# Giving each DMA engine its own partitions in the split x loads of a pairwise bilinear kernel

## Chip, cores and metric

The kernel runs on one core of one Trainium2 chip. The metric is the device time of one execution in microseconds (us). The core has a matrix engine (TensorE, in the profile PE), VectorE (DVE), ScalarE (ACT), GpSimd (POOL) and SyncE (SP); ACT, POOL and SP here only issue DMA transfers, apart from four constants that POOL writes at the start. The transfers of all three run on the same 16 DMA engines, numbered 0 to 15.

## What is computed

For 4096 samples with 32 fields of 64 numbers each, every pair of fields (i < j, 496 pairs) has its own 64 x 64 matrix W; the result is the product of field i with that matrix, multiplied elementwise with field j.

```python
i_idx, j_idx = np.triu_indices(32, k=1)
vi = inputs[:, i_idx, :]            # (4096, 496, 64)
vj = inputs[:, j_idx, :]
vdotw = jnp.einsum('bpd,pde->bpe', vi, W)
out = (vdotw * vj).reshape(4096, -1)
```

All is in float32. The output is 520 MB, the inputs together 42 MB.

## The kernel before

**Tiling.** The 4096 samples are cut into 8 chunks of 512 (`BANK`). The host puts x into a layout where a field pair is one block of 128 partitions (two fields of 64) by 512 samples; there are 16 such blocks. W lies in SBUF for the whole run, loaded at the start by SP in five pieces. For each chunk the steps (`steps_of`) go through the blocks in four groups of four (`GROUP`): first the pairs inside a group's blocks (L206), then each block p of the group with the later blocks q (L216). The matmuls write PSUM banks, VectorE multiplies them with x (L226, L234) and writes into one of three SBUF slots of 20, 18 and 18 blocks of 512 columns. When a slot is full SP stores it (L179): 4.6 or 5.1 MB per transfer. The next use of a slot waits for its store.

**The x loads.** x of a chunk is in one SBUF buffer of 128 partitions, half of it blocks 0 to 7, half blocks 8 to 15. Once the second group of a chunk is done, nothing in that chunk reads the first half again, and the first half of the next chunk is loaded there, while groups three and four go on; the second half follows after the last group. A half is 128 rows of 16 KB, 2 MB. As a rule a half is one transfer from ACT with all 128 partitions (L140), called a whole load here.

**The four split loads.** In chunks 1, 3, 5 and 7 (`LIGHT_CHUNKS`) the first half is loaded by `load_beside` instead, so that DMA engine 4 (`LIGHT`) moves none of its rows. It consists of two transfers from POOL: one over 15 engines, from engine 5 on and around to engine 3, 8 rows each (`HEAD`), partitions 0 to 119 in order; and one over two engines, 4 rows each (`REST`), partitions 120 to 127. The pair of engines changes from load to load (`PAIRS_FROM`: 7 and 8, 15 and 0, 1 and 2, 7 and 8). In DRAM the host writes one line for each engine, with 16 numbers (`PAD`) of padding behind it.

**Which engine a POOL transfer starts at.** [...] `from_engine(e)` moves this position: it issues a tiny transfer over as many engines as are to be skipped, called a nudge, into one of two small tiles that nothing reads. A nudge is issued as early as its place in POOL's order allows, which is the order of the program. So POOL's queue, for each split load, is: (nudge, issued long before) pair, nudge, the 15 engine transfer, nudge for the next split load.

**Order around the change.** ACT issues nothing but x loads, in program order, SP only W and the stores. Each waits on semaphores for the work that last read or wrote its place. A transfer takes a completion semaphore from a small rotating set, one set of eight for ACT and SP together, one of eight for POOL, and waits until the semaphore's last user is complete.

Of the kernel before, what the change touches and what calls it, by code (L numbers as in the profile page):

```python
# [8 lines left out]
F32 = mybir.dt.float32  # L9
ALU = mybir.AluOpType  # L10

P = 128
# [7 lines left out]
DMA_ENGINES = 16  # L20
LIGHT = 4
LIGHT_CHUNKS = [1, 3, 5, 7]
PAIRS_FROM = [7, 15, 1, 7]
HEAD = P // DMA_ENGINES
REST = HEAD // 2
PAD = 16


# [33 lines left out]
def is_light(load):  # L62

    return load[1] == 0 and load[0] in LIGHT_CHUNKS


def load_size(load):

    pads = (DMA_ENGINES + 1) * PAD if is_light(load) else 0
    return P * (load[2] - load[1]) * GROUP * BANK + pads  # L70


# [1 line left out]
def pair_bilinear_kernel(  # L74
# [10 lines left out]
    nc = tc.nc  # L85
# [5 lines left out]
    const = ctx.enter_context(tc.tile_pool(name="const", bufs=1))  # L91
    psum = ctx.enter_context(tc.tile_pool(name="ps", bufs=1, space=bass.MemoryType.PSUM))

    nudges = [const.tile([DMA_ENGINES, 16], F32, tag=f"nudge{i}", name=f"nudge{i}") for i in range(2)]
    cursor = 0

    def from_pool(out, in_):

        tc.keep_in_program_order(nc.gpsimd.dma_start(out=out, in_=in_))  # L99

    def from_engine(e):

        nonlocal cursor
        k = (e - cursor) % DMA_ENGINES
        if k:
            nudge = nudges[e == LIGHT + 1]
            from_pool(
                nudge[:k].rearrange("p (h c) -> p h c", h=2)[:, :, :4],
                x[: k * 8].rearrange("(p h c) -> p h c", p=k, h=2),
            )  # L110
        cursor = e

    def load_beside(at, xt, n_row, lap):

        nonlocal cursor
        most = DMA_ENGINES - 1
        for e, k, rows, p in (
            (PAIRS_FROM[lap], 2, REST, most * HEAD),
            (LIGHT + 1, most, HEAD, 0),
        ):  # L120
            from_engine(e)
            n = rows * n_row
            lines = x[at : at + k * (n + PAD)].rearrange("(k c) -> k c", k=k)
            from_pool(xt[p : p + k * rows], lines[:, :n])
            at += k * (n + PAD)
            cursor = (e + k) % DMA_ENGINES

    xbuf = const.tile([P, NPR * BANK], F32, tag="x", name="x")
    loads = x_loads(B, NPR)
# [1 line left out]
    def load_x(load):  # L131

        at = sum(load_size(before) for before in loads[: loads.index(load)])
        c, g0, g1 = load
        n = (g1 - g0) * GROUP * BANK
        xt = xbuf[:, g0 * GROUP * BANK : g0 * GROUP * BANK + n]
        if is_light(load):
            load_beside(at, xt, n, LIGHT_CHUNKS.index(c))
        else:
            nc.scalar.dma_start(out=xt, in_=x[at : at + P * n].rearrange("(p c) -> p c", p=P))  # L140

    for load in loads:
        if load[0] == 0:
            load_x(load)
# [40 lines left out]
    for c in range(NC):  # L185
        todo = list(enumerate(steps))
        while todo:
            if made == base + room:
                turn += 1
                base, room = made, SLOTS[turn % len(SLOTS)]  # L190
                tag = f"slot{turn % len(SLOTS)}"
                osb = ring.tile([P, room * BANK], F32, tag=tag, name=tag)
            (s, (p, q)), rest = todo[0], todo[1:]
            n = 1
# [28 lines left out]
            if q is None:  # L223
                for h in range(2):
                    rows = slice(h * D, (h + 1) * D)
# [21 lines left out]
            for load in loads:  # L247
                if last and load[0] == c + 1 and load[2] == p // GROUP + 1:
                    load_x(load)
# [55 lines left out]
```

## Time and profile before

| | us |
|---|---|
| median of 3 runs (1312.45 to 1314.46) | 1313.95 |
| the profiled execution | 1313.7 |
| its span in the profile | 1311.9 |
| VectorE busy | 1152.9 |
| PE busy | 1061.7 |
| a split load, POOL's issue to landing: the 15 engine transfer | 31.1 to 32.6 |
| the same: the pair | 12.1 to 13.9 |
| a whole 2 MB load from ACT, issue to landing, median | 20.9 |
| a 4.6 MB store, issue to landing, median | 23.6 |
| POOL's first transfer of each split load is issued at | 124.67, 447.29, 765.93, 1089.13 |
| the first matmul of the chunk that needs it starts at | 167.74, 491.37, 810.90, 1133.99 |

How to read it: the page gives busy time per engine over the span, the span in 40 slices, and the DMA queues (q1 is SP's, q10 ACT's, q0 POOL's; "instruction" is the fetching of the program itself). A stretch is a window of the span, given in us from its start, with the busy time of each engine, the share of the 16 DMA engines' time that was in use and the bytes moved per time. Landing is the time from a transfer's issue to its completion. The trace holds a record for every packet of every DMA queue, with its start, duration and size, but without the number of its engine; each row of a transfer here is one packet.

### The profile page before, as it was taken

The numbers are of one execution on the slowest core, as the hardware profiler recorded it, in microseconds if no ns is written. First come the engines' busy times: TensorE is split into PE (matmuls) and PEld (weight loads), VectorE is DVE, ScalarE is ACT, GpSimd is POOL, SyncE is SP. The second block draws the span as 40 slices with busy tenths as digits, with TensorE's granted clock in tenths as the row PEclk, the third lists the DMA queues.
The fourth block names the chain that finished last, engine by engine and source line by source line (L and its number), as shares of the span: only waits on it lengthen the run. The fifth ranks groups of instructions, "written<-read, shape, count | busy, mean of one in ns | idle before, by whom it ended". The sixth has DMA issues, their size and how long they took to land.

```text
span 1311.9 us, 9391 instructions
## 1 busy us (share of the span) xinstructions
PE 1061.7 (81%) x4096; PEld 402.1 (31%) x4096; DVE 1152.9 (88%) x725; POOL 9.4 (1%) x20
## 2 busy tenths in 40 slices
PE   6788778888878888799777887788888888878882
PEld 2333223333333323333233322233333333323330
DVE  6998789998899879999889987899889998899993
POOL 0000000000000000000000000000000000000000
PEclk9999899998999989999899998999989999999996
DMA  9999999999999999999999999999999999999998
GB/s 391 428 440 431 421 431 432 433 431 435 433 433 431 431 429 433 430 431 430 432 432 436 434 424 423 434 433 432 432 430 434 436 430 424 432 428 435 433 429 368
DMA packets 19625, 562.39 MB, mean 429 GB/s; under 512 B 2688, under 2 KB 2688, under 8 KB 2816
## 3 DMA queue, kind: packets, MB, share of 16 engines
q1 hardware_dynamic: 16560, 528.23, 93.6%
q10 hardware_dynamic: 1872, 25.17, 4.5%
q0 software_dynamic: 1152, 8.39, 1.6%
q8 instruction: 32, 0.52, 0.1%
q14 instruction: 9, 0.07, 0.0%
HBM read 41.68 MB, written 520.09 MB: 428 GB/s over the span
## 4 chain that ended last, share of the span: by engine, by line
DMA 56%; DVE 33%; PE 7%; issue 2%; DVEq 0%
DMA out_dram<-slot 56%; DVE slot L234 30%; PE pring L216 6%; DVE slot L226 3%; PE pring L206 1%; DMA x<-in_x_dram 1%; DVEq L234 0%; DVEq L295 0%; DVEq L226 0%
## 5 line engine op out<-in xcount | busy, mean ns | idle before, releaser
L234 DVE TENSOR_TENSOR slot<-pring,x 128x1024 f32<-128x1024 f32 (+1 forms) x661 | 1077.2, 1697 | 120.8 <-DMA out_dram<-slot 75.3
L216 PE MATMUL pring<-x,w 64*128 64x512 f32 x3840 | 997.3, 628 | 212.4 <-DVE slot L234 202.9
L216 PEld LDWEIGHTS pring<-x,w 64*128 64x128 f32 x3840 | 385.7, 191 | 822.1 <-DVE slot L234 503.2
L226 DVE TENSOR_TENSOR slot<-pring,x 64x1024 f32<-64x1024 f32 x64 | 77.9, 1217 | 16.0 <-PE pring L206 15.5
L206 PE MATMUL pring<-x,w 64*64 64x512 f32 x256 | 67.8, 652 | 12.9 <-DMA x<-in_x_dram 7.7
L206 PEld LDWEIGHTS pring<-x,w 64*64 64x64 f32 x256 | 16.4, 143 | 62.2 <-issue 30.2
L99 POOL DMA_DIRECT2D x<-in_x_dram x8 | 4.7, 586 | 1080.3 <-DVE slot L234 759.9
L99 POOL DMA_DIRECT2D nudge<-in_x_dram x8 | 4.6, 569 | 0.9 <-POOLq L291 0.9
L291 POOL MEMSET const-bfloat16-1.0<- 128x1 bf16 x1 | 0.1, 101 | 0.0
L291 POOL MEMSET const-float32-0.0<- 128x1 f32 x1 | 0.1, 98 | 0.2 <-issue 0.2
L291 POOL MEMSET const-float32-1.0<- 128x1 f32 x1 | 0.1, 98 | 0.0
L291 POOL MEMSET const-uint8-127<- 128x1 uint8 x1 | 0.1, 98 | 0.0
## 6 DMA issues: line engine op xcount, KB each, us to landing
out_dram<-slot SPq DMA_DIRECT2D x68, 4608.0 KB, 23.6
out_dram<-slot SPq DMA_DIRECT2D x35, 5120.0 KB, 22.6
x<-in_x_dram ACTq DMA_DIRECT2D x11, 2048.0 KB, 20.9
out_dram<-slot SPq DMA_DIRECT2D x4, 2560.0 KB, 21.6
x<-in_x_dram POOLq DMA_DIRECT2D x4, 1920.0 KB, 31.6
out_dram<-slot SPq DMA_DIRECT2D x2, 2048.0 KB, 22.7
w<-in_w_dram SPq DMA_DIRECT2D x1, 2816.0 KB, 30.0
x<-in_x_dram ACTq DMA_DIRECT2D x2, 1024.0 KB, 9.2
```

Source lines behind the costliest of these rows:

```text
L99: tc.keep_in_program_order(nc.gpsimd.dma_start(out=out, in_=in_))
L206: nc.tensor.matmul(pm[o * D : (o + 1) * D, ts(k, BANK)], w_sb[m * D : (m + 1) * D, s * P + k * D : s * P + (k + 1) * D], x_of(pair, m), st ...
L216: nc.tensor.matmul(pm[:, ts(2 * i + k, BANK)], w_sb[m * D : (m + 1) * D, ts(s + i, P)], x_of(p, m), start=True, stop=True,)
L226: nc.vector.tensor_tensor(strided(osb[rows, a : a + BANK], [BANK, 2]), strided(pm[rows, :BANK], [BANK, 2]), strided(x_of(p + 1 - h, h), [2 ...
L234: nc.vector.tensor_tensor(strided(osb[:, a : a + BANK], *blocks_of), strided(pm[:, :BANK], *blocks_of), strided(x_of(q), [BANK, n], [0, 2] ...
L291: nc = bacc.Bacc("TRN2", target_bir_lowering=False, num_devices=1)
```

## The change

Each of the four split loads now has eight parts in place of two, the same in all four. The engines 5 to 7 and 8 to 15 get, from POOL, [...] in two parts each (one per block of four partitions): 5 to 7 with three engines and 12 partitions, 8 to 15 with eight engines and 32 partitions. Engines 0 to 3 get theirs in two parts from ACT, four engines and 16 partitions each. Engine 4's eight partitions go two rows each to engines 7 and 8 (48 to 51, from POOL, first) and to a last two engine transfer from ACT (16 to 19). `PAIRS_FROM`, `HEAD` and `REST` go, and so does the argument `lap`.

The order per load is: POOL pair, ACT part, POOL nudge of 12, POOL 5 to 7, POOL 8 to 15, ACT part, POOL nudge of 5, POOL 5 to 7, POOL 8 to 15, ACT pair, and then a nudge of 7 for the next split load. There are thus three nudges per load, eight POOL transfers and three from ACT; before, two nudges, four POOL transfers and none from ACT. The nudges take their target in turn from three tiles. The host writes one padded line per engine and part: 34 lines per split load, before 17. The instructions of PE and VectorE, and the order of SP's stores, stay as they were.

```diff
-PAIRS_FROM = [7, 15, 1, 7]
-HEAD = P // DMA_ENGINES
-REST = HEAD // 2
+REST_FROM = 7
+QUAD = 4
...
+def light_parts():
+
+    own = LIGHT * QUAD
+    parts = [(REST_FROM, 2, own + P // 4, QUAD // 2)]
+    for p in (0, P // 4):
+        parts.append((None, LIGHT, p, QUAD))
+        parts.append((LIGHT + 1, 7 - LIGHT, p + own + QUAD, QUAD))
+        parts.append((8, 8, p + P // 2, QUAD))
+    parts.append((None, 2, own, QUAD // 2))
+    return parts
...
-    nudges = [const.tile([DMA_ENGINES, 16], F32, tag=f"nudge{i}", name=f"nudge{i}") for i in range(2)]
-    cursor = 0
+    nudges = [const.tile([DMA_ENGINES, 16], F32, tag=f"nudge{i}", name=f"nudge{i}") for i in range(3)]
+    cursor = turns = 0
...
-            nudge = nudges[e == LIGHT + 1]
+            nudge = nudges[turns % len(nudges)]
+            turns += 1
...
-    def load_beside(at, xt, n_row, lap):
+    def load_beside(at, xt, n_row):
 
         nonlocal cursor
-        most = DMA_ENGINES - 1
-        for e, k, rows, p in (
-            (PAIRS_FROM[lap], 2, REST, most * HEAD),
-            (LIGHT + 1, most, HEAD, 0),
-        ):
-            from_engine(e)
+        for e, k, p, rows in light_parts():
             n = rows * n_row
-            lines = x[at : at + k * (n + PAD)].rearrange("(k c) -> k c", k=k)
-            from_pool(xt[p : p + k * rows], lines[:, :n])
+            lines = x[at : at + k * (n + PAD)].rearrange("(k c) -> k c", k=k)[:, :n]
             at += k * (n + PAD)
-            cursor = (e + k) % DMA_ENGINES
+            if e is None:
+                nc.scalar.dma_start(out=xt[p : p + k * rows], in_=lines)
+            else:
+                from_engine(e)
+                from_pool(xt[p : p + k * rows], lines)
+                cursor = (e + k) % DMA_ENGINES
...
-            k = (DMA_ENGINES - 1) * HEAD
-            for part in (rows[k:].reshape(2, -1), rows[:k].reshape(DMA_ENGINES - 1, -1)):
-                x.append(np.pad(part, ((0, 0), (0, PAD))).ravel())
+            for _, k, p, n in light_parts():
+                x.append(np.pad(rows[p : p + k * n].reshape(k, -1), ((0, 0), (0, PAD))).ravel())
```

More of the change, by code (lines that the diff above doesn't have):

```diff
@@ L64, in is_light @@
     return load[1] == 0 and load[0] in LIGHT_CHUNKS
+def light_parts():
[7 more added lines that the diff above has]
+    return parts
 def load_size(load):
-    pads = (DMA_ENGINES + 1) * PAD if is_light(load) else 0
+    pads = sum(k for _, k, _, _ in light_parts()) * PAD if is_light(load) else 0
     return P * (load[2] - load[1]) * GROUP * BANK + pads
@@ L101, in from_engine @@
     def from_engine(e):
-        nonlocal cursor
+        nonlocal cursor, turns
         k = (e - cursor) % DMA_ENGINES
         if k:
-            nudge = nudges[e == LIGHT + 1]
+            nudge = nudges[turns % len(nudges)]
+            turns += 1
             from_pool(
@@ L137, in load_x @@
         if is_light(load):
-            load_beside(at, xt, n, LIGHT_CHUNKS.index(c))
+            load_beside(at, xt, n)
         else:
```

## The prediction

> **What bounds the kernel now.** I read the page first (engine shares, the slices, the queues), then the stretches around the four split x loads, then the waits of VectorE, then the landings, and last the packet records of the DMA queues.
>
> ```profile
> span 1311.9 us, 9391 instructions
> PE 1061.7 (81%) x4096; PEld 402.1 (31%) x4096; DVE 1152.9 (88%) x725; POOL 9.4 (1%) x20
> ...
> DMA  9999999999999999999999999999999999999998
> GB/s 391 428 440 431 421 431 432 433 431 435 433 433 431 431 429 433 430 431 430 432 432 436 434 424 423 434 433 432 432 430 434 436 430 424 432 428 435 433 429 368
> DMA packets 19625, 562.39 MB, mean 429 GB/s; under 512 B 2688, under 2 KB 2688, under 8 KB 2816
> ...
> q1 hardware_dynamic: 16560, 528.23, 93.6%
> q10 hardware_dynamic: 1872, 25.17, 4.5%
> q0 software_dynamic: 1152, 8.39, 1.6%
> q8 instruction: 32, 0.52, 0.1%
> ```
>
> The 16 DMA engines are full in every slice but the last; VectorE is at 88%. So the end is set by the DMA engine that finishes last, and each byte is moved once already. What is left is packets that take longer than they need, and engines that end at different times. The stretches show the first (columns: busy of PE, weight loads, VectorE, POOL, TensorE clock, DMA share, GB/s):
>
> ```profile
> 130.00:160.00 30.00, 22.90 (x81) 8.17 (x82) 23.91 (x16) 0.00 (x0) 0.90 1.00 420
> 200.00:280.00 80.00, 68.80 (x284) 27.00 (x280) 78.04 (x48) 0.00 (x0) 0.99 1.00 433
> 1094.00:1124.00 30.00, 23.96 (x88) 9.50 (x88) 23.88 (x16) 0.00 (x0) 1.00 1.01 424
> 1300.00:1306.00 6.00, 0.00 (x0) 0.00 (x0) 0.00 (x0) 0.00 (x0) 0.50 0.87 375
> 1306.00:1312.00 6.00, 0.00 (x0) 0.00 (x0) 0.00 (x0) 0.00 (x0) 0.50 0.25 107
> ```
>
> The engines are as busy in the first and third row as in the second, but move 420 and 424 GB/s, not 433: those are two of the four split loads. The last rows are the engines ending one after the other.
>
> The packet records say which. A 36,864 B store row takes 1364 ns, a 16,384 B load row 611 ns, almost always. The excess over that, summed over all engines, is 13.3, 3.1, 11.2 and 10.5 us during the four split loads, and 0.2 to 3.8 us (mean 1.7) during the ten later whole loads. A packet starts about 3 ns before its engine's previous one ends, and every store gives each engine eight rows, so the packets can be chained into 16 engines; the load and nudge packets tell which is which. Ends, in us before the last one:
>
> ```
> engine                        end        extra work in the whole run
> 4 (no split load rows)        0.0        its store rows take about 24 ns longer each, 20 us in all
> eight of 5,6,9 to 14          0.0, 2.2 to 4.2    four 16 KB instruction packets each, some 1.33 us apiece
> 7, 8                          1.5, 3.2   8 rows each, 4.9 us
> 0, 1, 2, 15                   4.1 to 5.3 4 rows each, 2.4 us
> 3                             2.6        none
> ```
>
> Within the split loads engine 4 lost 4.0 us, the other engine that ends last 2.7, the rest 0.7 to 2.8.
>
> [...] during a split load store rows and POOL's packets alternate, and even a 4-byte POOL packet waits one store row.
>
> **The change, part by part.**
>
> *Bytes.* The same 2 MB per load, engine 4 still has none. Engines 7, 8, 0, 1 get two rows more per load than the others: 4 x 2 x 0.61 = 4.9 us each. Engines 7 and 8 had that already; 0 and 1 go from 2.4 to 4.9; 2 and 15 from 2.4 to 0. None of 0, 1, 7, 8 gets instruction packets (four times 1.33 = 5.3 us), so no engine has more work than the fullest had.
>
> [...] If the excess falls to that of whole loads, 38.1 - 4 x 1.7 = 31 us goes, 1.9 us for each engine. What counts is the last ones. The instruction engine that ended last would end 2.7 us earlier, the others with their own split-load loss taken off 4.5 us or more before the old end; 7 and 8 about 4.0 to 4.5; engines 0 and 1 ended 4.1 to 5.3 us before, get back 1.8 to 2.7 and take 2.4 of new rows: 3.4 to 6 us before. Engine 4 is the open one: partitions 16 to 19 and 48 to 51[...] are still written by others, now 7 and 8 together and then 0 and 1, eight rows a load as before. [...] I take 2.5: the average foreign row in all cost 38.1/512 = 0.07 us, which would be 2.4 us for 32 rows. So engine 4 ends 1.5 us earlier and stays last.
>
> *Small packets.* From POOL a DMA puts on every engine outside it as many 4-byte packets as the engines in it get rows, and one more at its end. Before: pair 4+1, nudge 1+1, the big one 8+1 and the next nudge. After, on engines 8 to 15 until the last x part has landed: 3 for the pair, 2, 5, 1, 2, 5, 1 small ones (19) and 8 rows. Each small packet takes its engine some 6 ns net, and there are 11 to 19 more per load: 0.3 to 0.5 us, on every engine. I take 0.35.
>
> *Landing.* The first row starts 5.9 us after the issue. Turns: small 1.37 us, row 1.98 us. Before: 5.9 + 8 x 1.37 + 8 x 1.98 = 32.7; the DMA answers for the windows of two of the loads say 31.1 and 32.6 (KB, us to landing):
>
> ```profile
> x<-in_x_dram POOLq DMA_DIRECT2D x1, 1920.0 KB, 31.1
> ...
> x<-in_x_dram POOLq DMA_DIRECT2D x1, 1920.0 KB, 32.6
> ```
>
> The timeline has the next chunk's first matmuls, the waits have VectorE's (us in all, times, longest):
>
> ```profile
> 167.74 1.93 PE L206 MATMUL pring<-x,w 64*64 64x512 f32 x8
> ```
> ```profile
> DVE slot L234 <- DMA out_dram<-slot: 75.3, 48, 5.3
> ```
>
> After: 5.9 + 19 x 1.37 + 8 x 1.98 = 47.7 us. POOL issues at 124.67, and the next chunk's first matmul is at 167.74, 43.1 us later (44 to 45 in the other three). So where the load was 11 us early, PE now waits 3 to 5 us for x, and VectorE behind it nearly as long. This costs the end nothing as long as the stores in flight cover it: a store lands 23 us after its issue and takes about 10.8 us of the engines, so some 12 us of older stores stand ahead of it, and VectorE, which now waits 75.3 us in all for stores (last line), makes up 4 us in about one slot cycle.
>
> *Waits and issues.* ACT's three parts wait for the same VectorE and PE work as POOL's first, then each for a completion semaphore last used by a store several stores back. Behind them on ACT stands only the whole load some 45 us later. They take three of the eight semaphores that SP's stores also use in turn; the first store to reuse one is the fifth after, over 40 us later, when a part with ten rows (a whole load: eight rows in 20.9 us) is long in. POOL issues eight DMAs at 0.57 us, not four; nothing follows on it, but 2.3 us more belongs to the landing's upper end. The third nudge target only keeps a nudge from waiting for the last; nothing waits for it. PE and VectorE instructions are unchanged, SP's order too.
>
> **Sum.** 4.0 - 2.5 - 0.35 = 1.15 us off the profiled execution (1313.7 us, span 1311.9 and 1.8 around it); the median of the runs shown is 1313.95, so 1312.8.
>
> **Rivals.**
> - *Full gain.* Engine 4 loses next to nothing to its eight foreign rows, and the last engines end 2.5 to 4 us sooner: 1310.0 to 1311.5, say 1310.8. For it: whole loads show little excess in several cases. Against: engine 4's stores are the one place where foreign rows stay.
> - *No gain.* [...] 1313.5 to 1317.5, say 1315. For it: in the fourth load, where engine 7 was one of the pair, engine 4 lost half of its 4.0 us.
> - *Slower: the late load.* The place is the start of every other chunk; the price is the stall beyond what stores in flight cover. It decides from a landing about 55 us after the issue (44 + 11). If POOL's eight DMAs or three queues on an engine stretch it to 57, each of four loads costs 2 us: 1321. For it: the landing grows by half in my own count. Against: 7 us are left, and the first engines to run dry are not the last ones.
> - *Other engines than meant.* If ACT's parts fell on engine 4, up to 40 rows x 0.61 = 24 us more on the last engine: 1337. [...]
>
> **How the numbers follow.** The forecast 0.52, full gain 0.27, no gain 0.11, late load 0.08, other engines 0.02. This kernel can tell about 0.2%, 2.6 us, from no change, that is 1311.3 to 1316.6. Faster: 0.24 of full gain, and 0.06 of the forecast where engine 4 keeps 1 us or less. Slower: 0.10 and 0.02 of no gain. Same: the rest, 0.58. The range takes in full gain and no gain, 1309.8 to 1317; late load and wrong engines are left out.
>
> **What would show it.** Right: excess in the split loads near that of whole ones, except on engine 4's stores; stretches at 430 GB/s or more; the last x part landing 45 to 50 us after POOL's issue and a PE wait of 3 to 5 us on x at four chunk starts; VectorE waiting less for stores and more for PE. Wrong: excess unchanged[...], a DMA share under 1.00 after a chunk start (the late load), load rows on engine 4.

## The result, and the profile after

The changed kernel takes 1323.24 us (median of 6 runs, 1322.76 to 1324.85), the kernel before 1312.57 (6 runs, 1311.16 to 1314.46). The ratio is 1.0082, with a 95% interval of 1.0069 to 1.0095: 10.7 us slower. The forecast was 1312.8, the range ended at 1317.0. The profiled execution has 1323.3 us and a span of 1321.5, 9.6 us more than before.

These are the lines of the page of the changed kernel that answer to those shown of before: span and engines, DMA share and GB/s in 40 slices, packets, and the queues (packets, MB, share of 16 engines).

```profile
span 1321.5 us, 9454 instructions
PE 1064.7 (81%) x4096; PEld 407.0 (31%) x4096; DVE 1153.2 (87%) x725; POOL 18.0 (1%) x36
...
DMA  9999999999999999999999999999999999999998
GB/s 391 439 430 429 427 422 430 433 421 435 425 437 430 420 427 419 431 433 423 430 423 436 430 422 422 427 432 429 424 428 427 429 435 423 422 433 431 435 429 353
DMA packets 20513, 562.39 MB, mean 426 GB/s; under 512 B 3576, under 2 KB 3576, under 8 KB 3704
...
q1 hardware_dynamic: 16560, 528.23, 93.5%
q10 hardware_dynamic: 2056, 27.53, 5.0%
q0 software_dynamic: 1856, 6.04, 1.2%
q8 instruction: 32, 0.52, 0.1%
```

The bytes are the same and the 16 engines are as full as before, yet they move 426 GB/s, not 429. So no engine stood idle; packets took longer. 888 packets more are small ones (3,576 for 2,688 under 512 B).

Where they took longer is seen in stretches. First two of the kernel before (498 to 514 us and 982 to 998 us), each for the most part inside a whole load, which the change doesn't touch; columns as in the prediction, the last two being DMA share and GB/s:

```profile
498.00:514.00 16.00, 14.07 (x56) 5.29 (x57) 16.00 (x11) 0.00 (x0) 1.00 1.02 436
...
982.00:998.00 16.00, 13.75 (x56) 5.47 (x53) 15.54 (x10) 0.00 (x0) 0.96 1.02 434
```

Then the changed kernel: a split load, a quiet stretch with stores alone, the same two stretches with whole loads, a split load again, and the end.

```profile
130.00:160.00 30.00, 22.43 (x80) 7.63 (x78) 22.27 (x16) 0.00 (x0) 0.89 1.00 425
...
200.00:280.00 80.00, 66.19 (x274) 25.16 (x274) 76.39 (x48) 0.00 (x0) 1.00 1.00 432
498.00:514.00 16.00, 15.23 (x50) 6.04 (x46) 11.51 (x8) 0.00 (x0) 0.77 1.00 415
...
982.00:998.00 16.00, 13.01 (x54) 5.44 (x54) 15.00 (x11) 0.00 (x0) 1.00 1.00 404
...
1094.00:1124.00 30.00, 25.52 (x88) 12.49 (x84) 23.68 (x15) 3.87 (x7) 0.89 1.01 423
...
1306.00:1312.00 6.00, 0.00 (x0) 0.00 (x0) 0.00 (x0) 0.00 (x0) 0.50 0.98 423
1312.00:1318.00 6.00, 0.00 (x0) 0.00 (x0) 0.00 (x0) 0.00 (x0) 0.50 0.53 225
```

The quiet stretch is as fast as before (432 for 433). Most of the loss is in the whole loads, 415 and 404 GB/s for 436 and 434, at a DMA share of 1.00: transfers that the change left as they were.

The size of these differences is rough. A packet counts where it starts, so that one store row on each engine, 16 x 36,864 B, is 37 GB/s of a stretch of 16 us, and the second load starts 9 us later in the changed kernel (987 for 978 us). A rate from the packet records is free of such edges: the bytes of all packets that start during the ten later whole loads, over the time of these packets per engine. It is 428.9 GB/s before and 417.9 after; from here on it is called the rate of the ten loads.

The packet records give it in numbers. "Excess" is, as in the prediction, the time of packets over what one of their size usually takes, summed over 16 engines; from here on only packets at least 80 ns over are counted, the start of the kernel with the load of W is left out, and 390 ns is taken off for each instruction packet that falls in (the store row behind one takes 368 to 412 ns longer). In one execution each:

```
excess, us                        before    after
in the four split loads             31.6     51.1
in the ten later whole loads        14.6     99.9
elsewhere                            3.8     15.1
```

The sum grows from 50.0 to 166.1 us, 7.3 us for each engine, and the small packets add 0.5 us to each (32.2 for 24.4 us over 16 engines). That is most of 9.6 us. Mostly store rows are hit: of 8,704 rows of 36,864 B, 251 are 80 ns or more over 1364 ns, before 99. The median stays at 1364 ns.

The waits for x and for the stores, in us in all, times, longest; first PE's wait for x in the kernel before, then both in the changed one:

```profile
PE pring L206 <- DMA x<-in_x_dram: 7.7, 1, 7.7
...
DVE slot L245 <- DMA out_dram<-slot: 81.0, 46, 5.5
...
PE pring L217 <- DMA x<-in_x_dram: 16.0, 5, 7.6
```

Of the 16.0 us, 7.6 are the wait at the start of the kernel, which was there before (7.7); 8.4 are new, at the four chunk starts that the split loads feed (2.0, 3.8, 2.4 and 0.2).

### The profile page after: what moved, and what is told of

Its sections match the earlier page's. It is cut to its first block, busy times and chain, and to the rows that moved or that the text cites. A ratio compares the mean times of both kernels' runs of the same rounds, so it can differ in the third digit from the quotient of the medians.

```text
span 1321.5 us, 9454 instructions
## 1 busy us (share of the span) xinstructions
PE 1064.7 (81%) x4096; PEld 407.0 (31%) x4096; DVE 1153.2 (87%) x725; POOL 18.0 (1%) x36
## 2 busy tenths in 40 slices
DMA packets 20513, 562.39 MB, mean 426 GB/s; under 512 B 3576, under 2 KB 3576, under 8 KB 3704
## 3 DMA queue, kind: packets, MB, share of 16 engines
q10 hardware_dynamic: 2056, 27.53, 5.0%
q0 software_dynamic: 1856, 6.04, 1.2%
## 4 chain that ended last, share of the span: by engine, by line
DMA 55%; DVE 34%; PE 6%; issue 2%; POOL 1%; DVEq 0%
DMA out_dram<-slot 41%; DVE slot L245 32%; DMA x<-in_x_dram 14%; PE pring L227 5%; DVE slot L237 2%; PE pring L217 1%; POOL x L110 1%; POOL nudge L110 0%; DVEq L245 0%; DVEq L305 0%
## 5 line engine op out<-in xcount | busy, mean ns | idle before, releaser
L227 PEld LDWEIGHTS pring<-x,w 64*128 64x128 f32 x3840 | 389.8, 192 | 816.8 <-DVE slot L245 498.3
L217 PE MATMUL pring<-x,w 64*64 64x512 f32 x256 | 73.8, 657 | 22.5 <-DMA x<-in_x_dram 16.0
L110 POOL DMA_DIRECT2D x<-in_x_dram x20 | 11.1, 564 | 1080.4 <-DVE slot L245 757.6
```

The lines of the kernel that those rows point to most:

```text
L217: nc.tensor.matmul(pm[o * D : (o + 1) * D, ts(k, BANK)], w_sb[m * D : (m + 1) * D, s * P + k * D : s * P + (k + 1) * D], x_of(pair, m), st ...
L227: nc.tensor.matmul(pm[:, ts(2 * i + k, BANK)], w_sb[m * D : (m + 1) * D, ts(s + i, P)], x_of(p, m), start=True, stop=True,)
```

## The experiments

Each ran together with the kernel before on one chip. Ratios are to it, with 95% intervals; excess is of one execution. An expectation that names a letter means: Q, partly filled transfers on ACT's queue disturb what follows; A, the addresses in DRAM (the padding); S, where tiles start in SBUF. Which partitions are an engine's own is an assumption of the author: the record of a packet names neither its engine nor its partitions.

### First round: ACT's transfers, padding, filling

**Three small ACT transfers in the kernel before.** Per split load three of them, over 4, 4 and 2 engines, into three small tiles of their own.

```diff
+    sides = [const.tile([4, 16], F32, tag=f"side{i}", name=f"side{i}") for i in range(3)]
...
+        for side, k in zip(sides, (4, 4, 2)):
+            tc.keep_in_program_order(nc.scalar.dma_start(
+                out=side[:k].rearrange("p (h c) -> p h c", h=2)[:, :, :4],
```

> The kernel before, with three tiny transfers from ACT (4, 4 and 2 engines, 64 B a row, into tiles that nothing reads) at each split load. Theory Q (a transfer from ACT over fewer than 16 engines changes how ACT's later whole loads are spread): the excess over the usual packet duration in the ten whole loads rises from 15 us, summed over engines, to about 100 us, and the time by some 5 us to 1318. Theory A (where the rows of x lie in DRAM, moved by the padding, decides the excess): no change, 1313, excess of the whole loads under 25 us.

Measured: 1.0064 [1.0047, 1.0081], whole-load excess 64.6 us. It looked like a proof that ACT's partial transfers are the cause. It was none, as the second round shows.

**Padding.** `PAD` 32 in the kernel before gives its lines the total padding of the change; `PAD` 8 in the changed kernel gives that of before.

```diff
-PAD = 16
+PAD = 32
```

> The kernel before with PAD 32 in place of 16, so that each split load carries 2176 B of padding, as in the changed kernel, and what follows in DRAM lies where it does there. Theory A: the excess in the whole loads rises to about 100 us and the time to about 1318 to 1320. Theory Q: no change, 1313.

> The changed kernel with PAD 8 in place of 16: 1088 B of padding for each split load, as in the kernel before, so that the whole loads read the same addresses as before. Theory A: the excess in the whole loads falls from 100 us to about 15 to 25 us and the time from 1323 to about 1316. Theory Q: no change, 1323.

Measured: 0.9998 [0.9987, 1.0008] and 1.0066 [1.0051, 1.0081]. The padding makes no difference beyond these intervals (the change itself: 1.0082 [1.0069, 1.0095]).

**Filling up.** The changed kernel with one more ACT transfer per split load, over six engines, so that the engines counted by ACT's partial transfers come to 16.

```diff
+    side = const.tile([6, 16], F32, tag="side", name="side")
```

> The changed kernel with one more tiny transfer from ACT over 6 engines at the end of each split load, so that the engines of ACT's partial transfers of a load add up to 16. Theory Q, if ACT's next transfer starts where the last ended: the whole loads' excess falls to about 15 us and the time to about 1316. Theory A: no change, 1323, whole loads at 100 us.

Measured: 1.0071 [1.0056, 1.0086], whole-load excess 108.5 us. No help.

### Second round: where the tiles stand in SBUF

The three slow kernels of the first round had one thing in common with the change that no theory had named: each has small tiles more than before. A nudge tile is 64 B in each partition, and x, W and the store slots stand behind them. The compiled programs have x at byte 16,640 of a partition before (65 x 256, a multiple of 256 B) and at 16,704 after, with W and the slots moved alike. In the kernel with three side tiles it is 192 B past a multiple, in the filled one 128 B.

**The kernel before with one nudge tile that nothing uses**, the single word 3 for 2 in the list of nudge tiles:

```diff
-... name=f"nudge{i}") for i in range(2)]
+... name=f"nudge{i}") for i in range(3)]
```

> The kernel before with a third nudge tile that nothing uses. Each such tile is 64 B of each partition, so x, W and the store slots start 64 B further on in SBUF: x at 16,704 and not 16,640, which is 65 times 256. No transfer is added or changed. Theory S (the start of x and the slots in SBUF against multiples of 256 B decides the excess during x loads): the excess in the ten whole loads rises from 15 us to about 100 us, and the time to about 1321, as in the changed kernel, which has the same addresses. Theory Q (partial transfers from ACT): no change, 1313.

Measured: 1.0067 [1.0044, 1.0091]. No transfer is added or taken away, all keep their order, only the places in SBUF differ, and most of the loss is there. The quiet stretch and the two stretches with whole loads of this kernel:

```profile
200.00:280.00 80.00, 68.24 (x280) 25.84 (x276) 76.90 (x47) 0.00 (x0) 0.99 1.00 433
498.00:514.00 16.00, 14.56 (x60) 5.73 (x56) 15.94 (x12) 0.00 (x0) 1.00 1.01 417
...
982.00:998.00 16.00, 13.12 (x46) 5.16 (x44) 13.42 (x10) 0.00 (x0) 0.89 1.00 400
```

It is the picture of the changed kernel: 433 where only stores run, 417 and 400 beside loads. The rate of the ten loads is 419.9 GB/s.

**The changed kernel with three more unused nudge tiles**, six in all: x, W and slots are on multiples of 256 B again; the nudges use three of them, as in the change.

```diff
-... name=f"nudge{i}") for i in range(3)]
+... name=f"nudge{i}") for i in range(6)]
...
-            nudge = nudges[turns % len(nudges)]
+            nudge = nudges[turns % 3]
```

> The changed kernel with three more tiles of 64 B that nothing uses (three are still used in turn), so that x starts at 16,896 = 66 x 256 and the slots at multiples of 256. Theory S: the excess of the whole loads falls to about 15 us, that of the split loads below the 32 us of the kernel before, and the time to about 1312 to 1314, which is then what the change of the loads alone is worth. Theory Q: no change, 1323.

Measured: 1.0017 [1.0010, 1.0024]. Four fifths of the loss are gone. Its split and whole loads:

```profile
130.00:160.00 30.00, 22.11 (x84) 7.72 (x84) 23.20 (x16) 0.00 (x0) 0.94 0.99 425
...
498.00:514.00 16.00, 13.98 (x56) 5.20 (x54) 15.97 (x11) 0.00 (x0) 1.00 1.03 433
...
982.00:998.00 16.00, 13.84 (x62) 5.80 (x58) 15.05 (x11) 0.00 (x0) 1.00 0.99 413
```

The DMA share of 1.03 in the second line shows the edge at work: 433 is too high. By the packet records the two loads run at 418 and 416 GB/s, for 425 and 426 before and 413 and 408 in the change, and all ten at 424.9. The 1312 to 1314 us expected were not reached (1315.9): something is left.

**The three ACT transfers again, with a fourth side tile** so that the addresses are as before.

```diff
-... name=f"side{i}") for i in range(3)]
+... name=f"side{i}") for i in range(4)]
```

> The kernel before with the three tiny transfers from ACT at each split load again, and one more unused tile, so that x starts at a multiple of 256 (16,896). Theory S: as before, 1313 to 1314, whole loads under 25 us of excess. Theory Q: 1322, as without the unused tile.

Measured: 1.0002 [0.9993, 1.0011], excess in split and whole loads 18.9 and 7.1 us. The same transfers cost nothing; in the first round it was their tiles.

**Only the slots moved.** The kernel before with an unused 64 B tile between W and the slots; x and W stay.

```diff
+    const.tile([P, 16], F32, tag="gap", name="gap")
```

> The kernel before with 64 unused bytes between W and the store slots: x and W start at multiples of 256 as before, the slots 64 B past one. If theory S acts through the stores' reads of SBUF: the time rises to about 1320 and most of the 100 us of excess in whole loads is there. If it acts through the loads' writes: 1313, under 25 us. Theory Q: 1313.

Measured: 1.0062 [1.0043, 1.0081]. **Only x and W moved**, in the third round: a third nudge tile, and 192 B behind W to put the slots right.

```diff
-... name=f"nudge{i}") for i in range(2)]
+... name=f"nudge{i}") for i in range(3)]
...
+    const.tile([P, 48], F32, tag="gap", name="gap")
```

> The kernel before with a third, unused nudge tile and an unused 192 B tile behind W: x and W start 64 B past a multiple of 256 B in SBUF, the store slots stand on a multiple again. If the cost of the shift comes only through the stores' reads of the slots, this is the kernel before: ratio 0.999 to 1.002, whole-load excess under 25 us. If the loads' writes into x cost as well, the ratio is 1.003 to 1.007 and the whole-load excess 50 to 80 us.

Measured: 0.9995 [0.9987, 1.0003]. The two whole loads with only the slots moved:

```profile
498.00:514.00 16.00, 14.80 (x60) 6.17 (x60) 15.59 (x11) 0.00 (x0) 0.99 0.99 399
...
982.00:998.00 16.00, 13.16 (x48) 5.21 (x46) 13.46 (x10) 0.00 (x0) 0.89 1.00 412
```

and with only x and W moved:

```profile
498.00:514.00 16.00, 13.95 (x59) 5.65 (x60) 16.00 (x12) 0.00 (x0) 1.00 1.02 435
982.00:998.00 16.00, 13.10 (x58) 5.47 (x57) 14.41 (x11) 0.00 (x0) 1.00 0.99 420
```

399 and 412 against 435 and 420; rate of the ten loads 421.6 against 427.4 GB/s; whole-load excess 66.1 against 22.5 us. So it is the start of the slots, which the stores read, and not the start of x, which the loads write. VectorE writes the slots, but it is as fast with them moved (1153.5 us busy, before 1152.9).

### Third to fifth round: what is left, 0.17%

**DRAM once more, at 256 B.** `PAD` 64 makes every line start on a multiple of 256 B in DRAM as well, in the kernel before and in the aligned changed one.

> The kernel before with PAD 64, so that lines of x and W start on a multiple of 256 B in DRAM too. If only the SBUF side counts, nothing changes: ratio 0.998 to 1.002. If the DRAM side of a load costs anything of the same kind, the time falls by 2 us or more (ratio under 0.9985) and the packets of loads become shorter than 1364 ns.

> The changed kernel with x, W and slots on multiples of 256 B (three more unused nudge tiles) and PAD 64. If only the SBUF side counts it is the aligned changed kernel again: ratio 1.001 to 1.0025. If the DRAM side counts in loads of whole rows by single engines, it falls to 0.999 or below.

Measured: 1.0001 [0.9993, 1.0009] and 1.0019 [1.0013, 1.0026]. Nothing changes. (The 1364 ns of the first expectation belong to a store row; a load row takes 611 ns in the kernel before.)

**Even rows.** In the aligned changed kernel the rows counted as engine 4's, 16 to 19, go one each to engines 0 to 3, and the other four to 7 and 8 or to 15 and 0 in turn.

```diff
-    parts = [(REST_FROM, 2, own + P // 4, QUAD // 2)]
+    parts = [(REST_FROM[LIGHT_CHUNKS.index(c)], 2, own + P // 4, QUAD // 2)]
...
-    parts.append((None, 2, own, QUAD // 2))
+    parts.append((None, LIGHT, own, 1))
```

> The aligned changed kernel, with the four rows that engine 4 gives up in each split load (16 to 19) taken one each by engines 0 to 3 instead of two each by two engines, and the four rows of the rest dealt out to other engines over the four loads, so that no engine's sum of rows is more than 4 rows over another's. If what is left of the loss (1.0017) is the uneven sum of extra rows, the ratio falls to 0.998 to 1.000. If it is not, it stays at 1.001 to 1.0025.

Measured: 1.0020 [1.0012, 1.0028]. The uneven sums are not it.

**Small packets without the change.** The kernel before (slots aligned) with six more nudges of eight engines in every split load: in the first kernel behind the last part, in the second between the pair and the 15 engine transfer.

```diff
+    def skip_round():
+
+        for nudge in nudges[2:8]:
+            from_pool(
+                nudge[:8].rearrange("p (h c) -> p h c", h=2)[:, :, :4],
```

> The kernel before, with six more nudges of eight engines each after the last x part of every split load: about 12 more small packets on every engine per load, as in the change, with x landing as early as before. x, W and slots on multiples of 256 B. If the small packets are the rest of the loss: ratio 1.001 to 1.0025. If it is the later landing or whose partitions are written: 0.999 to 1.0008, that is 0.3 to 0.5 us for the packets themselves.

> The kernel before, with the same six nudges between the pair and the 15 engine transfer: the same small packets, and x lands some 14 to 17 us later, 45 to 48 us after POOL's issue, as in the change. If the later landing is the rest of the loss: ratio 1.001 to 1.0025, and whole-load excess over 35 us, where the kernel with the nudges behind has under 25. If not: 0.999 to 1.0008.

Measured: 1.0017 [1.0011, 1.0024] behind, 1.0032 [1.0023, 1.0042] ahead. Six more nudges, which are twelve more small packets on each engine per load (20,393 packets in all for 19,625), are enough for 0.17%, 2.2 us, though the packets' own time is only 0.4 us an engine. The later landing came out close to what was wanted: PE's waits for x end 47.7, 48.4, 47.7 and 50.5 us after POOL's first issue. But PE waits longer than in the change; the wait for x in the second kernel:

```profile
PE pring L216 <- DMA x<-in_x_dram: 45.5, 5, 10.8
```

Without the 7.5 us at the start that is 38.0 us at four chunk starts, where the changed kernel has 8.4 and the aligned one 1.5. The 0.15% between the two kernels is thus a bound for the late load in the change, and their intervals just meet. The expected whole-load excess over 35 us was missed: 22.8 (20.5 with the nudges behind).

**Other partitions.** The aligned changed kernel with the same transfers, but all partitions turned by 64.

```diff
-    return parts
+    return [(e, k, p ^ (P // 2), rows) for e, k, p, rows in parts]
```

> The aligned changed kernel with the partitions of all parts turned by 64 (p becomes p xor 64): the same transfers on the same engines in the same order[...]. If writing its own partitions is what took the split loads' excess down[...], the excess goes back to 25 to 45 us from 12 to 17, and the ratio to 1.002 or more. If it is not: excess 10 to 20 us and ratio 1.001 to 1.0025, as in the aligned changed kernel.

Measured: 1.0034 [1.0021, 1.0047] (5 runs), excess in the split loads 32.5 us, where the aligned changed kernels have 12.0, 17.4 and 17.5. So which engine gets which partitions may count, as the prediction assumed. It rests on single executions, and these scatter: the old split loads, which by the same assumption write other engines' partitions too, have from 18.9 to 46.1 us in the table below. In time it is about 0.17%, with intervals of two rounds that overlap.

**Fewer POOL transfers.** Own partitions as in the change, the rows counted as engine 4's all from ACT, two nudges and four parts from POOL.

```diff
-    parts = [(REST_FROM, 2, own + P // 4, QUAD // 2)]
+    parts = []
...
+        parts.append((None, LIGHT, p + own, 1))
-    parts.append((None, 2, own, QUAD // 2))
```

> Own partitions for 0 to 3 and 5 to 15 as in the change, but engine 4's eight rows go one each to engines 0 to 3 in each block, from ACT; POOL is left with two nudges of five engines and four parts per load, six transfers and not eight, and about 16 small packets on an engine of 8 to 15 and not 24. x, W and slots on multiples of 256 B. If small packets, landing and own partitions add up: 0.17% x 6/12 for packets, some 0 to 0.05% for a landing at about 41 us, less 0.17%: ratio 0.9985 to 1.0000. If the gain of own partitions shows only beside the slower delivery: 1.001 to 1.002.

Measured: 1.0046 [1.0033, 1.0058]. The sum of parts that I had made from the last three kernels fails here: fewer small packets, no wait of PE for x after the start, and yet slower. Its runs lie far apart (1316.9 to 1323.3 us), and the profiled one is the fastest of them, so the trace doesn't show what the slow ones lost.

What the traces have in common is in this table (excess in us, one execution each):

```
kernel                               ratio     split loads   whole loads
before                               1             31.6          14.6
ACT transfers, aligned               1.0002        18.9           7.1
only x and W moved                   0.9995        42.9          22.5
nudges behind                        1.0017        45.9          20.5
nudges ahead                         1.0032        46.1          22.8
change, aligned                      1.0017        12.0          40.2
  the same, PAD 64                   1.0019        17.4          49.2
  the same, even rows                1.0020        17.5          45.1
  the same, turned by 64             1.0034        32.5          44.0
  fewer POOL transfers               1.0046        20.2          44.4
```

In all five kernels with split parts like the change's the whole loads, which are the old ones, lose 40 to 49 us, in the others 7 to 23. Where the split loads save something, some 11 to 20 us, more than that is lost again there. Small packets, late landing, uneven rows, DRAM addresses and whose partitions are written don't bring it about by themselves, since the kernels that have one of them alone, or lack it, don't follow it. Why the split parts make later whole loads worse stays open.

The table sets ratios of many runs beside the excess of one execution, and not each of these is typical: the one with ACT transfers, aligned, is the fastest of its 12 runs (1311.8 us), the one with only x and W moved the slowest of its 12 (1316.1). Nor does the excess account for the last 0.17%. In the profiled execution of the aligned changed kernel (1316.3 us, the one of before 1313.7) all excess together is 6 us above that of before (56.0 for 50.0), 0.4 us for each engine, and the small packets take 0.5 us more. That leaves more than half of the 2.6 us, so this loss stays open too.

No version beat the kernel before.

## Why the prediction was wrong

- **What bounds the kernel**: right. The engines are full before and after, and the end moved with the duration of packets.
- **Which engine does what**: right as far as the records show, in which packets have to be chained into engines. One engine got no load rows in a split load, before as after (before, two got 12 rows and thirteen 8); ACT's parts went to the four engines without POOL rows (10, 10, 8 and 8 rows per load); and 2.36 MB moved from POOL's queue to ACT's (q0 8.39 to 6.04, q10 25.17 to 27.53).
- **The third nudge target**: this is the step that failed. The prediction put it as "only keeps a nudge from waiting for the last; nothing waits for it" and priced it at nothing. The edit of one number moves everything behind the nudge tiles by 64 B, takes the store slots off a multiple of 256 B, and alone costs 0.67% (8.8 us of 1313.6). With the shift undone the change costs 0.17%; 1.0067 x 1.0017 = 1.0084, measured 1.0082. No case had a tile's place in it, and so the range couldn't hold the time.
- **Own partitions**: single executions speak for them, their worth was not got. Aligned, the split loads' excess falls from 31.6 to 12 to 17 us; turned by 64 it goes back to 32.5. Why, no run shows, nor that rows in engine 4's partitions cost it the 4.0 us: the 2.5 us of the sum was an estimate, and what engine 4 lost was not taken out of the records again. And the sum (4.0 less 2.5) took it for granted that the untouched whole loads stay as they are. They went from 14.6 to 40 us and more, and the total with everything else from 50.0 to 56.0.
- **Small packets**: 0.35 us per engine. Their own time grew by 0.5, close enough. But about as many in the old kernel, put there with six more nudges per load, cost 2.2 us at the end: pricing them at their own time was too low.
- **Landing**: 47.7 us after POOL's first issue. By the packet records the last row ended after 43.1, 45.3, 44.9 and 43.3, and PE's waits for x ended after 46.9, 47.5, 47.7 and 47.0; so the sum was right, though in the kernel before the first row starts 4.6 to 5.1 us after the issue on the profile's clock, not 5.9. PE's wait of 3 to 5 us was 0.2 to 3.8. That this costs the end nothing is not refuted for a wait of this size (the bound is 0.15% for one of four times the length). VectorE was to wait less for stores; it waited 81.0 us for 75.3, since the stores were slower.
- **Full gain, no gain, late load, other engines**: none of them. The late load had the right sign and about the right time (1321), which is luck: what would have shown it, a DMA share that falls after a chunk start, is missing. The queues' shares add up to 99.8% of the span after as before.

A cost on every store row would have shown where only stores run. But in the changed kernel the median row takes 1364 ns, as before, and the quiet stretch runs at 432 GB/s for 433; with the 64 B alone it is 433.

## What to carry to other kernels

When a diff adds, drops or resizes any SBUF tile, look at where the tiles behind it start, above all those that large stores read: try these on multiples of 256 B, as here (64 B off cost 0.62 and 0.67%), and put small tiles in numbers that keep it, or behind the big ones. An experiment that adds a small tile of its own changes two things at once; give it a twin that has the tile without the operation. A gain in one kind of transfer on full DMA engines is a gain at the end only if the untouched transfers keep their durations (in the aligned change the split loads' excess fell from 31.6 to 12.0 us, that of the whole loads rose from 14.6 to 40.2), so count those as well.

## What the runs showed of the hardware

- Stores that read SBUF rows starting 64, 128 or 192 B past a multiple of 256 B lose 0.6 to 0.8% of this kernel, all kernels with that shift alike (1322.1 to 1323.6 us). The shift by 64 B was run alone (1.0062, 1.0067), those by 192 and 128 B only together with small ACT transfers, the second in the changed kernel; in the kernel before such transfers cost nothing where the slots are aligned (1.0002). They lose it beside loads: the rate of the ten whole loads is 417.9 to 421.6 GB/s for 428.9 in the change and in the two kernels with the 64 B alone, while stores alone, from 200 to 280 us, run at 432 to 433 either way. How the shift and a running load act together no run shows.
- Loads that write SBUF rows starting 64 B past such a multiple lose nothing (0.9995 [0.9987, 1.0003]). The start of a line in DRAM makes no difference beyond the intervals at 32, 64, 128 or 256 B of padding: in the kernel before 0.9998 and 1.0001 with 128 and 256 B against its own 64, in the change 1.0066 with 32 for 1.0082 with 64, in the aligned change 1.0019 with 256 for 1.0017 with 64.
- Six extra nudges in each of four loads, twelve small packets on each engine per load, cost 2.2 us at the end (behind the last part, 1.0017 [1.0011, 1.0024]; ahead of the 15 engine transfer 1.0032 [1.0023, 1.0042], with PE waiting longer for x) with 0.4 us of packet time on each engine.
